# Reordering the small matrix products that stand behind the hidden rounds of a two-layer convolution kernel

## The chip, the core and the metric

The kernel runs on one core of a Trainium2 chip. The core has five engines that each work through a queue of their own: TensorE (PE in the profile, with its weight loads as PEld), VectorE (DVE), ScalarE (ACT), GpSimd (POOL) and SyncE (SP, which here only issues DMAs). Times are device microseconds of one execution. "Time" is the median of several executions; the profile is one further execution with the hardware profiler on.

## What is computed

The input x is 8 images (batch elements) of 8 channels and 512 x 512 values, all in 32-bit floats. Two residual layers follow each other.

```
# layer 0
v  = group_norm(x, 4 groups of 2 channels)
F  = rfft2(v[:, :, ::2, ::2]);  keep 8 x 4 low modes
G  = einsum('bixy,ioxy->boxy', F, w1 or w2)      # complex mixing of channels
x  = x + real(inverse transform of G at 512 x 512)
# layer 1
v  = group_norm(x)
grid = v
for _ in range(15):
    mapped  = 3.9 * grid * (1 - grid)
    grid    = 0.85 * (0.7 * mapped + 0.3 * conv3x3_depthwise(mapped)) + 0.15 * v
cml  = clip(grid)
nca  = sigmoid(conv1x1(relu(conv3x3(v, 8 -> 128)), 128 -> 8))
g    = sigmoid(conv1x1(relu(conv3x3([v, cml, nca], 24 -> 8)), 8 -> 8))
x  = x + g * cml + (1 - g) * nca
```

## The kernel before

The whole program is unrolled by a Python planner that writes every engine's instructions in one fixed order. Five kinds of work are interleaved.

- **Steps.** The 15-step loop runs on slabs of rows. `Slabs.convolve` (L535) writes one step as 48 matrix products into one half of PSUM; `Slabs.settle` (L548 on VectorE, L554 on ScalarE) reads the result and squares it. `settle` is called on two halves of a tile, so a step has two L548 instructions and two L554. After a step POOL issues small transfers (L581, L582) that renew the rows at the seams between slabs, and SP stores one row block (L591, `past`) for the last slab of a half.
- **Hidden rounds.** `Hidden.round` (L734) computes 128 hidden channels for 4 rows into one half of PSUM; ScalarE (L740) reads its first part and VectorE (L742) the second, into a tile `h`. `Hidden.point` (L761) multiplies `h` by the 1 x 1 weights; rounds in groups of four share one output tile `y`, which a ScalarE copy (L768) starts, VectorE adds to (L770), and a sigmoid closes (L773).
- **Gates.** A `Gate` handles 12 rows of the last stage. `load` issues six transfers on SP (three into `gin`, L796, and three into `mix`, L801). `conv` (L811, with L817 and L821 on VectorE and L816 on POOL), `point` (L828, with the sigmoid L832 on ScalarE and L834 on POOL) and `finish` (L839 on VectorE and the store L846 on SP) follow.
- **Layer 0 of the next element** is a generator, `layer0`. At each `yield` it names the kind of place at which its next piece may run. Its pieces are: statistics and the row transform of each of the 8 channels (`BATCH_NORM_STATS2` L332 on VectorE, products L338, copy L343); two averagings over partitions for the group norm (`group_stats`, L303 twice, with the square root L316 on ScalarE between its end and what follows); the column transform (L364); the complex mixing (`total`, L375 to L381, called once for the real part and once for the imaginary part, then L393 to L396, which fill `om`); and for each channel a product over rows (`over_rows`, L404, copied by L409), two products that add the result to x (`synthesis`, L437 and L440), new statistics (L457), and for each pair of channels a `close`: again two averagings, the square root, and the normalisation of both channels (L418, L421), after which they are stored.
- **The turn.** `work` emits one "tick": three steps, up to three hidden rounds, and then what stands behind the rounds. There are about 45 ticks for an element.

PSUM has eight banks, held as four pairs; two pairs make a half. Steps and rounds take the two halves in turn, so a step cannot begin to write a half before the step or round that used it last has been read by VectorE and ScalarE. Behind the rounds the names `first` and `second` stand for the two halves. If layer 0 has a WIDE piece (the synthesis) it takes the half that is next in turn, which becomes `second`, and `first` is the half of the last round. If not, `first` is the half of the round before last and `second` that of the last round. In both cases the next tick's first step writes `second`. (If two gates are convolved in a tick, it writes `first`.) Before the change the order behind the rounds is:

1. WIDE piece in `second`;
2. if the rounds belong to two groups, `point` of the older group in `first[1]`;
3. a gate's `conv` in `first[0]`, if one is loaded;
4. an EARLY piece of layer 0 in `second[0]`;
5. a second gate's `conv` in `second[0]`, if one is loaded;
6. `point` of the younger group in `first[1]`, a FILL piece (no PSUM);
7. up to two LATE pieces, in `second[1]` and `second[0]`;
8. `point` of the gates, then loads for further gates.

A closing's first averaging is EARLY and its second averaging is LATE. In the mixing, the real part is LATE and the imaginary part is EARLY one tick later; the first `over_rows` is LATE in that same tick.

`gates` is the number of gates to be loaded in a tick: 0, 1 or, when an element has more rows left than open ticks, 2. With 2, `work` loads one gate after the first step of the tick, and one at the tick's end. `shared.most` is the number of large buffers that gates and layer 0 may hold together: 4 as a rule, 3 near the ends of phases, and 7 from the sixth step slot of an element's first half to that half's end.

## Time and profile before

| What | Value |
|---|---|
| median of 3 runs | 9339.16 us (9327.55 to 9340.95) |
| the profiled execution | 9328.59 us, of which the span from the first to the last instruction is 9326.8 us |
| TensorE busy | 8776.0 us, 94% of the span |
| VectorE, ScalarE, GpSimd busy | 61%, 44%, 36% |
| mean granted TensorE clock | 0.987 |
| DMA | 1327 MB, mean 142 GB/s |

TensorE is the engine that sets the time: the span is its busy time and 551 us (9326.8 less 8776.0) of idle time, most of it in short pieces. A line of the waits view says which instruction waited, for whom, for how long in total, how often, and how long at most. A line of the timeline has the start and the length in us, the engine, the source line, what is written and read, the shapes and the number of instructions, and in brackets the idle time before the first of them with its releaser. One matrix product of the source stands as two records (103680 records for 1080 steps of 48 products), so the three steps of a tick are "x288".

### The profile page before, as it was taken

The page shows a single profiled execution, that of the slowest core. Times are in us where ns is not written, and L with a number is a line of the kernel's source. Part 1 is how long each engine was busy: PE and PEld are TensorE (multiplying, and loading weights), DVE is VectorE, ACT ScalarE, POOL GpSimd, SP SyncE. Part 2 cuts the span into 40 slices and gives each one's busy share as a digit, 9 for nine tenths or more (in the row PEclk, how much of TensorE's full clock was granted, in tenths as well). Part 3 has the DMA queues.
Part 4 walks back from the last instruction along what each step waited for, and adds up shares of the span by engine and source line. Part 5 has one row for each costly group of instructions (what it writes and reads, how often), then busy time and mean ns, then how long its engine had stood idle before and what let it go on. Part 6 is the DMA issues. An engine that isn't in the chain of part 4 may idle for free. (4 is left out here: it accounts for less than half of the span.)

```text
span 9326.8 us, 334742 instructions
## 1 busy us (share of the span) xinstructions
PE 8776.0 (94%) x150992; PEld 4165.1 (45%) x150992; DVE 5685.6 (61%) x5844; ACT 4101.0 (44%) x4285; POOL 3378.9 (36%) x4441
## 2 busy tenths in 40 slices
PE   5999999999999999999999999999999999899988
PEld 2445544444444444444444444444444444344433
DVE  5665567556665567655676556755567555555655
ACT  2445444444444444444444444444444444344422
POOL 3242334334343243433334343343433324453422
PEclk9999999999999999999999999999999999999999
DMA  5241356745566455754657546575455755665487
GB/s 158 79 127 39 96 150 167 171 109 152 148 178 146 112 155 145 184 137 112 169 146 176 129 108 167 156 179 126 111 158 167 173 117 129 144 153 119 105 212 184
DMA packets 697414, 1327.26 MB, mean 142 GB/s; under 512 B 146939, under 2 KB 152443, under 8 KB 668499
## 3 DMA queue, kind: packets, MB, share of 16 engines
q1 hardware_dynamic: 591840, 1244.38, 51.8%
q0 software_dynamic: 101792, 60.33, 3.0%
q8 instruction: 1187, 19.45, 0.9%
q14 instruction: 241, 1.97, 0.1%
q10 hardware_dynamic: 2354, 1.14, 0.0%
HBM read 977.48 MB, written 270.61 MB: 134 GB/s over the span
## 5 line engine op out<-in xcount | busy, mean ns | idle before, releaser
L535 PE MATMUL pair<-m,band 32*32 32x512 f32 x103680 | 3669.8, 605 | 205.2 <-issue 132.7
L554 ACT ACTIVATE m<-m 128x1024 f32<-128x1024 f32 x2016 | 2128.8, 1056 | 2081.0 <-DVE m L548 1994.9
L535 PEld LDWEIGHTS pair<-m,band 32*32 32x32 f32 x103680 | 2166.3, 103 | 1664.5 <-issue 820.3
L734 PE MATMUL pair<-cols,w_p 32*128 32x511 f32 (+1 forms) x24576 | 2800.1, 596 | 64.3 <-DMA cols<-xn 36.0
L734 PEld LDWEIGHTS pair<-cols,w_p 32*128 32x128 f32 x24576 | 1311.0, 185 | 1565.4 <-issue 1189.8
L548 DVE SCALAR_TENSOR_TENSOR m<-pair,dO 128x1024 f32<-128x1024 f32 x1152 | 1356.9, 1219 | 1040.0 <-PE pair L535 772.5
L581 POOL DMA_DIRECT2D m<-m x1568 | 855.3, 545 | 3061.0 <-ACT m L554 2983.1
L742 DVE TENSOR_SCALAR h<-pair,b_p 128x1024 f32<-128x1024 f32 x1024 | 1311.9, 1283 | 1045.4 <-PE pair L734 1035.3
L548 DVE SCALAR_TENSOR_TENSOR m<-pair,dE 128x1024 f32<-128x1024 f32 x1008 | 1187.3, 1219 | 867.3 <-PE pair L535 635.3
L740 ACT ACTIVATE h<-pair,b_p 128x1024 f32<-128x1024 f32 x1024 | 1141.2, 1115 | 1206.6 <-PE pair L734 1196.6
L834 POOL TENSOR_TENSOR mix<-mix 96x512 f32<-96x512 f32 x344 | 451.0, 1317 | 2010.8 <-ACT mix L832 1958.3
L761 PE MATMUL pair<-h,w_u 128*32 128x512 f32 x8192 | 999.0, 597 | 56.9 <-DVE y L770 30.4
L811 PE MATMUL pair<-gin,w_g 128*32 128x511 f32 (+1 forms) x8256 | 963.2, 604 | 64.5 <-DMA gin<-nca 45.8
L582 POOL DMA_DIRECT2D m<-m x1568 | 840.5, 536 | 36.7 <-issue 30.7
L811 PEld LDWEIGHTS pair<-gin,w_g 128*32 128x32 f32 x8256 | 254.3, 111 | 721.2 <-issue 654.8
L761 PEld LDWEIGHTS pair<-h,w_u 128*32 128x32 f32 x8192 | 246.2, 110 | 674.6 <-issue 516.5
L816 POOL TENSOR_TENSOR mix<-mix 96x512 f32<-96x512 f32 x344 | 446.4, 1300 | 191.0 <-DMA mix<-nca 143.5
L773 ACT ACTIVATE y<-y,b_u 128x512 f32<-128x512 f32 x256 | 184.9, 722 | 748.2 <-DVE y L770 747.9
L768 ACT COPY y<-pair 128x512 f32<-128x512 f32 x256 | 149.9, 586 | 693.3 <-PE pair L761 686.0
L558 POOL TENSOR_SCALAR dO<-dO 128x2048 f32<-128x2048 f32 x72 | 398.1, 5529 | 88.1 <-DVE m L548 87.0
L817 DVE SCALAR_TENSOR_TENSOR mix<-mix,back 96x512 f32<-96x512 f32 x344 | 379.7, 1104 | 81.0 <-DMA mix<-nca 63.9
L821 DVE TENSOR_SCALAR mix<-pair,b_g 128x512 f32<-128x512 f32 x344 | 257.2, 748 | 248.2 <-PE pair L811 238.2
(91 smaller groups left out, 3023.6 us busy)
## 6 DMA issues: line engine op xcount, KB each, us to landing
gin<-xn SPq DMA_DIRECT2D x344, 384.0 KB
cols<-xn SPq DMA_DIRECT2D x256, 512.0 KB
x<-in_x SPq DMA_DIRECT2D x120, 1024.0 KB
gin<-cml SPq DMA_DIRECT2D x344, 320.0 KB
gin<-nca SPq DMA_DIRECT2D x344, 320.0 KB
dE<-xn SPq DMA_DIRECT2D x288, 256.0 KB
dO<-xn SPq DMA_DIRECT2D x288, 256.0 KB
mix<-xn SPq DMA_DIRECT2D x344, 192.0 KB
```

Source lines behind the costliest of these rows:

```text
L535: nc.tensor.matmul(ps[h // 2][32 * t : 32 * t + 32, h % 2], band[at, self.channel(step - 1, h, t), dx], m[at, t, dx : dx + N], start=(n == ...
L548: nc.vector.scalar_tensor_tensor(u[:, at], ps[q], FLOOR, d[:, at], ALU.max, ALU.add)
L554: nc.scalar.square(u[:, at], u[:, at])
L581: nc.gpsimd.dma_start(out=view(tb, rb, dims), in_=view(ta, ra, dims))
L582: nc.gpsimd.dma_start(out=view(ta, ra + s, dims), in_=view(tb, rb + s, dims))
L734: nc.tensor.matmul(ps[g // 2][:, g % 2, lo:hi], w_p[p, dx, i % 2], self.cols[p, i // 2, at : at + hi - lo], start=(n == 0), stop=(n == 2), ...
L740: nc.scalar.activation(h[:, :2], ps[0], AF.Relu, bias=b_p)
L742: nc.vector.tensor_scalar(h[:, 2:], ps[1], b_p, 0.0, ALU.add, ALU.max)
L761: nc.tensor.matmul(ps[32 * g : 32 * g + 32], w_u[:, r % 4], h[:, g], start=(r == hs[0][0]), stop=(r == hs[-1][0]), tile_position=(0, 32 * g),)
L811: nc.tensor.matmul(ps[32 * j : 32 * j + 32, lo:hi], gband[:, dx], gin[:, j, at : at + hi - lo], start=(n == 0), stop=(n == 2), tile_positi ...
L816: nc.gpsimd.tensor_tensor(d, d, ng, ALU.subtract)
L834: nc.gpsimd.tensor_tensor(d, d, mix[: GR * C, 2], ALU.mult)
```

## The change

Five edits are made in one diff.

- A new kind of place, LAST, stands after the gates' `point`; its PSUM is `first[1]`, which the next step does not write. The second averaging of `group_stats` moves to it, at all five calls for each element. LATE keeps one place, `second[1]`.
- The mixing becomes one FILL piece: real and imaginary part and the filling of `om` follow each other in one tick. The first `over_rows` becomes EARLY in the next tick.
- If no gate is ready in a tick, the EARLY piece runs first of all, before the `point` of either group, and in `first[0]`. If one is ready the order is as before.
- `conv` of `Others` no longer tests whether a gate is ready; `ready` does.
- With `gates == 2` the load after the first step is made only while `shared.most < 6`. Else both gates are loaded at the tick's end.

```diff
 in group_stats, before the second averaging:
-        yield LATE, None
+        yield LAST, None
 in layer0:
-        yield LATE, None
+        yield FILL, None
         re = total(0, 0, 1, 1, ALU.subtract, "re")
-        yield EARLY, None
         im = total(0, 1, 1, 0, ALU.add, "im")
...
         nc.vector.scalar_tensor_tensor(to[:, :, 4:8], im, on_cos, back, ALU.mult, ALU.add)
-        yield LATE, None
+        yield EARLY, None
...
             if closing:
-                yield LATE, None
+                yield LAST, None
                 next(closing, None)
                 closing = None
...
-        for kind in (EARLY, LATE):
+        for kind in (EARLY, LAST):
             yield kind, None
             next(closing, None)
 in Others:
+        def ready(self):
+            if not self.loaded or now[0] < self.hold:
+                return False
+            return self.loaded[0].at + self.lag <= now[0]
+
         def conv(self, ps):
-            if not self.loaded or now[0] < self.hold or self.loaded[0].at + self.lag > now[0]:
-                return False
             g = self.loaded.popleft()
             g.conv(ps)
             self.convolved.append((g, ps))
-            return True
 in work:
-            if gates == 2:
+            if gates == 2 and shared.most < 6:
                 others.load(1)
                 gates = 1
...
         groups = e.hidden.sums()
+        gate = others.ready()
+        if not gate:
+            others.spectral(EARLY, [first[0][:, 0]])
         if len(groups) == 2:
             e.hidden.point(groups.pop(0), first[1][:, 0])
-        others.conv(first[0][:, 0])
-        others.spectral(EARLY, [second[0][:, 0]])
-        two = others.conv(second[0][:, 0])
+        two = False
+        if gate:
+            others.conv(first[0][:, 0])
+            others.spectral(EARLY, [second[0][:, 0]])
+            two = others.ready()
+            if two:
+                others.conv(second[0][:, 0])
         if groups:
             e.hidden.point(groups[0], first[1][:, 1])
         others.spectral(FILL, [None])
-        others.spectral(LATE, [second[1][:, 0], second[0][:, 0]])
+        others.spectral(LATE, [second[1][:, 0]])
         others.point()
+        others.spectral(LAST, [first[1][:, 0]])
         used[0] += two
```

In the order of the built programs, 49 of the 361 stretches between one tick's steps and the next differ on TensorE: five to seven in each of the seven elements that have a layer 0 beside them, and two in the last element, where the run of ticks with two gates starts one tick later and ends one tick later. The order on SP differs only in that last place, and the number of matrix products, transfers and VectorE operations is the same.

More of the change, by code (lines that the diff above doesn't have):

```diff
@@ L55 @@
 TICK = 3
-WIDE, EARLY, FILL, LATE = "wide", "early", "fill", "late"
+WIDE, EARLY, FILL, LATE, LAST = "wide", "early", "fill", "late", "last"
 GATES_FROM, SPECTRAL_FROM = 1, 0
```

## The prediction

> **What bounds the kernel now.** The page gives PE 8776.0 us of 9326.8: the sum of PE's work sets the time, and an edit that moves no work off PE can win only idle time, 551 us. So I read the waits of PE first, then timelines where they stand.

> ```profile
> engine line waited for: us in total, times, longest us
> PE pair L535 <- issue: 132.7, 83, 4.5
> PE pair L811 <- DMA gin<-nca: 45.8, 15, 5.8
> PE pair L535 <- ACT std L316: 40.0, 25, 2.7
> ...
> PE pair L303 <- DVE var L313: 34.1, 14, 12.2
> PE pair L761 <- DVE y L770: 30.4, 35, 1.2
> ```

> Three rows bear on the edits: std and var (the second averaging) and gin (gates). The next lines are a tick of a typical later element with a closing, in PE's, VectorE's and ScalarE's timelines. The LATE averaging (L303) wrote `second`, so L535 waits until ScalarE has loaded a table and taken the root.

> ```profile
> 5925.95 0.22 PE L303 MATMUL pair<-var,avg 128*32 128x1 f32 x8
> 5926.01 1.04 PE L828 MATMUL pair<-mix,w_g 128*32 128x512 f32 x6
> 5928.42 9.73 PE L535 MATMUL pair<-m,band 32*32 32x512 f32 x287 [1.36 <-ACT std L316]
> ...
> 5928.60 2.61 DVE L421 TENSOR_SCALAR x<-x,mean,rstd 128x2048 f32<-128x2048 f32 x2
> 5931.82 2.36 DVE L548 SCALAR_TENSOR_TENSOR m<-pair,dO 128x1024 f32<-128x1024 f32 x2 [0.62 <-PE pair L535]
> ...
> 5926.81 1.28 ACT L316 ACT_TABLE_LOAD   x1
> 5928.10 0.26 ACT L316 ACTIVATE std<-pair,eps 128x1 f32<-128x1 f32 x1
> 5928.38 1.28 ACT L832 ACT_TABLE_LOAD   x1
> 5929.68 0.69 ACT L832 ACTIVATE mix<-pair,b_g 96x512 f32<-96x512 f32 x1
> ```

> Next, a tick without a gate: L770 frees the bank for the second `point` before the statistics L332 begin.

> ```profile
> 5693.91 0.48 PE L338 MATMUL pair<-dft_y,x 128*32 128x32 f32 x32
> 5694.90 1.06 PE L761 MATMUL pair<-h,w_u 128*32 128x512 f32 x8 [0.51 <-DVE y L770]
> ...
> 5694.16 0.69 DVE L770 TENSOR_TENSOR y<-y,pair 128x512 f32<-128x512 f32 x1 [0.59 <-PE pair L761]
> 5694.76 4.84 DVE L332 BATCH_NORM_STATS2 st<-x 128x6 f32<-128x512 f32 x8
> ```

> Last, a two-gate tick of the last element, and the sums over it (PE, PEld, DVE, ACT, POOL, then granted clock, DMA share, GB/s): the first conv doesn't wait, the second does, and then takes twice as long.

> ```profile
> 8007.29 2.78 PE L811 MATMUL pair<-gin,w_g 128*32 128x512 f32 x24
> 8015.17 4.99 PE L811 MATMUL pair<-gin,w_g 128*32 128x512 f32 x24 [5.11 <-DMA gin<-nca]
> ...
> 7993.00:8021.00 28.00, 22.89 (x387) 10.01 (x383) 12.67 (x13) 8.72 (x9) 10.79 (x16) 0.88 0.64 149
> ```

> [...] 4.99 against 2.78 us for the same 24 records, clock 0.88. [...] The trace shows the 1.28 and no drain (the root follows 0.01 us later); I use 1.28.

> **The change, part by part.** The built order says what moves. Times are us.

> *Closings with a gate* (four for each of the six later elements). L828 now comes before L303, and L535 need not wait, so steps start 1.36 earlier (5927.06). But ScalarE now runs L832 (0.69) ahead of the table load, and nothing else has shortened: L828 ends 5927.05, L832 5927.8, load 5929.1, root 5929.4 instead of 5928.36. Behind it VectorE has L318 to L421 (2.83), and only then L548 of step 1 (2.36): done at 5934.6. Step 3 needs that half free. At 3.24 a step it could start at 5927.06 + 6.49 = 5933.55 and so waits 1.1. Before, it started at 5934.91. Of 1.36, 0.26 remains: the stall moves from step 1 to step 3. The closing at 5976 gives 0.6 of its 1.84 by the same working, the one at 6030 0.26. The last closing has L472 and L473 (1.5) behind L421 too: there PE loses 0.7 where the clock held (6089), and gains about 1.7 where the clock had fallen during the 2.7 wait for var (granted 0.5 around 1572); I take 0.5. Four together: +1.6.

> *Front averaging* (5798): the 0.68 on var and about 0.5 on the root go, 0.5 comes back at step 3: +0.6.

> *Mixing as one piece*: 12 small VectorE operations in two ticks become one block. im to `om` (5843.98 to 5846.62, 2.64) moves ahead of L548 one tick earlier, under step 1: settle 1 ends 28.7 after 5800, step 3 could start 28.4, cost 0.3. In the next tick the 1.79 of L404 on `om` goes; L828 then starts at 5845.9 for 5847.56, since L404 is already done: +1.65. Together +1.35.

> *EARLY first without a gate.* With rounds in one group (5715), L338 no longer waits 1.26 on L740, as `first` is an older half; but the row statistics L332 (2.47) hold L770, L773 and the copy L343 that frees `second`: +0.4 remains. With two groups (5694) it costs: in the built order L332 x4 (2.47 from 5693.57) now stands ahead of L770, which starts at 5696.03 for 5694.16. The second L761 waits for it: -1.87.

> Each later element: 1.6 + 0.6 + 1.35 + 0.4 - 1.87 = +2.1; six of them **+12**.

> *The first element's neighbour* has no gates, so L832 isn't in the way. By the same walk: two ticks with two groups -3.7; the waits of 1.26 at 234, 256 and 322 give 0.4, 1.2, 1.2; the front averaging at 306, whose root also waits behind L773, +3; first L404 +1.85 (1.41 on `om` and 0.4 of y); closings at 421, 476, 531 and 579. At 476 and 531 L303 waited 1.70 each for L440 on `second`, which `first` avoids, so the root itself comes 1.2 or more sooner; PE ran at half clock there (granted 0.5 near 421, 469, 476, 524). I take 2.3, 4, 4 and 0.5. Sum **+15**.

> *Two gates at the tick's end.* Six ticks (7967.89 to 8134.44, mean 27.8). Their waits on the second gin sum to 3.57 + 5.11 + 3.38 + 4.45 + 5.25 + 3.60 = 25.4. Half clock follows: each slow L811 costs up to 2.2, so the ceiling is about 39. On SP the twelve transfers of both gates now follow the two stores (which wait for L839, 6.5 after the tick begins) and `past` L591 (8009.53, 14.7 after). They carry 2 x (384 + 320 + 320 + 3 x 192) KB = 3.2 MB. The first conv comes 9.75 + 2.6 after the next tick begins, so about 18 after `past` in a 20-us tick. At 149 GB/s for a share of 0.64, full use would be 233, and 3.2 MB takes 14 at the least, 18 at 0.78 of that. That just fits; it isn't seen in the trace. From 5 (bound by transfers) to 39 (free); I take **+27**.

> *At nothing*: the `ready` test (Python); the prologue, where every queue keeps its order and only the rotation of banks differs; and the sigmoid table, which stood to be loaded again before L832 (5928.38) and is now loaded before the next tick's L773 or L832. There ScalarE idles (5.54 before L768 in the tick shown)[...]; uncovered, it would cost up to 1.28 in ticks where L828's bank is the next one written, and these are not among them. The closings' stores are issued a tick later as before, and SP's order is the same there, so no transfer moves but those of the gates. L834 on POOL comes with L832 some 2 sooner; L839 waits for it, which can only help.

> **Sum.** 12 + 15 + 27 = 54 off the profiled execution's 9328.6: 9274.6. That execution lies 10.6 below the median; off 9339.2 the sum is 9285. I predict **9286**.

> **Rivals.**
> - *A: the closings give all back and the two-group ticks decide.* [...] For: L421 is 2.61 and cannot move. Elements then give 0 instead of 27: 9339 - 27 = 9312.
> - *B: transfers bound the two-gate ticks.* For: share 0.64 already in 28-us ticks, 0.9 in 20. Against: slices of the page reach 212 GB/s. Gate gain 5: 9339 - 27 - 5 = 9307.
> - *C, slower: the gates' loads arrive late as a bunch.* Place: SP behind L591. If all twelve need over 27 us (122 GB/s; 121 was the lowest among these ticks), both convs wait. Each tick then loses 9 of wait and 2.3 of clock, six times 11.3 or 68 for the 39 before. It decides from about 11 a tick; with the elements at 5: 9339 + 29 - 5 = 9363.
> - *D: all gate stalls go and every half-clock stretch with them*: 39 + 40: 9260.

> **How the numbers follow.** Forecast 0.60 (9268 to 9306, run scatter in it), A 0.13, B 0.14, C 0.06, D 0.07. The range 9260 to 9322 leaves out C, half of D and the tails of A and of run scatter. 0.2% is 18.7 us, about what can be told from no change: faster means below 9320.5. Faster: 0.58 + 0.08 + 0.11 + 0.07 = 0.84; same 0.11; slower 0.05.

> **What would show it.** Right: L535 on std nearly gone, but new waits of L535 on VectorE's m (L548) or short gaps 6 to 7 us after a closing tick begins; L761 on y near 2.4 in the eight two-group ticks; L404 on `om` gone; two L811 groups of 2.7 back to back between 7990 and 8140, clock above 0.95. Wrong: if L535 after closings runs 288 records in 9.75 us with no stall, the closings are worth 30 us more than I say; if L811 waits on gin before the *first* conv of these ticks, B or C holds.

## The result

The changed kernel takes 9276.02 us (median of 5 runs, 9257.73 to 9298.59) where the kernel before took 9333.21 in the same comparison (5 runs, 9319.23 to 9340.95): a ratio of 0.9938, interval 0.9925 to 0.9952. A second, later comparison (`after_again`, below) gave 0.9956, 0.9941 to 0.9972. The forecast was 9286 in a range of 9260 to 9322.

Line numbers above 384 are one lower in the changed kernel: the steps are L534, `settle` L547, `point` L760, `y` L769, `conv` L810, the gates' `point` L827 and L831, the normalisation L420.

### The profile after

The waits view of the changed kernel, TensorE only (who waited, for whom, us in total, times, longest):

```profile
engine line waited for: us in total, times, longest us
PE pair L534 <- issue: 135.8, 75, 4.4
PE pair L760 <- DVE y L769: 46.7, 36, 2.3
...
PE pair L810 <- DMA gin<-nca: 15.0, 8, 3.5
PE pair L303 <- DVE var L313: 14.1, 2, 12.2
...
PE pair L534 <- DVE m L547: 11.0, 6, 1.8
...
PE pair L534 <- ACT mys L343: 7.0, 7, 1.0
...
PE pair L534 <- ACT std L316: 0.5, 1, 0.5
```

The three targets are gone or cut: std 40.0 to 0.5, var 34.1 to 14.1 (12.2 of it is one wait in the prologue), gin 45.8 to 15.0. Three rows show what was paid: `y` rose from 30.4 to 46.7, L534 waits for VectorE's `m`, which is a new row, and its wait for the copy L343 rose from 2.7 to 7.0. The row "issue", the largest of all, hardly moved; a later section returns to it.

Timelines of the changed kernel: first a closing tick on TensorE, ScalarE and VectorE, then a tick without a gate and with two groups (TensorE, then VectorE), then the steps and the two convs of a two-gate tick:

```profile
5898.99 0.60 PE L827 MATMUL pair<-mix,w_g 128*32 128x512 f32 x3
5899.04 0.22 PE L303 MATMUL pair<-var,avg 128*32 128x1 f32 x2
...
5899.99 10.93 PE L534 MATMUL pair<-m,band 32*32 32x512 f32 x288
...
5900.13 0.68 ACT L831 ACTIVATE mix<-pair,b_g 96x512 f32<-96x512 f32 x1 [0.31 <-PE pair L827]
5900.83 1.28 ACT L316 ACT_TABLE_LOAD   x1
5902.13 0.26 ACT L316 ACTIVATE std<-pair,eps 128x1 f32<-128x1 f32 x1
...
5902.62 2.60 DVE L420 TENSOR_SCALAR x<-x,mean,rstd 128x2048 f32<-128x2048 f32 x2
5905.14 2.35 DVE L547 SCALAR_TENSOR_TENSOR m<-pair,dO 128x1024 f32<-128x1024 f32 x2
...
5664.05 0.46 PE L338 MATMUL pair<-dft_y,x 128*32 128x32 f32 x32
...
5668.61 1.07 PE L760 MATMUL pair<-h,w_u 128*32 128x512 f32 x8 [2.34 <-DVE y L769]
...
5665.41 2.46 DVE L332 BATCH_NORM_STATS2 st<-x 128x6 f32<-128x512 f32 x4
5667.79 0.67 DVE L769 TENSOR_TENSOR y<-y,pair 128x512 f32<-128x512 f32 x1
...
7972.53 4.52 PE L534 MATMUL pair<-m,band 32*32 32x512 f32 x128 [2.57 <-issue]
7980.23 1.51 PE L534 MATMUL pair<-m,band 32*32 32x512 f32 x17 [3.18 <-issue]
...
7985.69 5.35 PE L810 MATMUL pair<-gin,w_g 128*32 128x512 f32 x48
```

In the closing tick the steps begin at once behind L827, without a wait in brackets, but the 288 records take 10.93 us where three steps that wait for nothing take 9.73 to 9.75. The records' own start times say where: the first pieces of step 3 (records 192, 194 and 196, counted from 0) start at 5906.41, 5906.86 and 5907.54, where the records just before them start hundredths of a microsecond apart. L547 frees them between 5906.3 and 5907.5. Each piece alone is too short for the waits view; only the length of the group betrays the wait. In the two-gate ticks both convs run as one group of 48 at 2.7 us for 24 records (granted clock 1.00), as the first conv of before (2.78 at 1.00). But the steps of this tick stop twice on "issue", for 2.57 and 3.18 us, where no step of these ticks stopped before.

The windows view (busy time of PE, PEld, DVE, ACT, POOL, then granted clock, DMA share, GB/s) over the two-gate ticks, before and after; the stretches are not the same work, so only the last three columns are compared:

```profile
7966.00:8133.00 167.00, 138.59 (x2324) 60.95 (x2312) 87.43 (x85) 55.84 (x59) 63.58 (x88) 0.92 0.63 144
```

```profile
7966.00:8125.00 159.00, 149.46 (x2776) 67.74 (x2746) 96.40 (x96) 65.18 (x68) 69.91 (x97) 0.99 0.68 166
```

The clock rose from 0.92 to 0.99, and the transfers ran faster, 166 GB/s for 144, so they were not at their limit before.

Laid tick against tick, the two traces differ as follows (gain in us). In what follows, the time of "the steps" runs from a tick's first L534 to the first record behind them (9.68 where nothing waits); "behind" is the rest, the rounds and what follows them.

| Stretch | Predicted | Measured |
|---|---|---|
| the first element's neighbour (18 ticks) | 15 | 21.1 |
| the two-gate ticks and those beside them (11 ticks) | 27 | 25.7 |
| six later elements (18 ticks each) | 12 | 11.4 |
| everything else | 0 | -5.6 |
| span | 54 | 52.6 |

The third row depends on where a stretch is cut, since stops on "issue" are scattered over it: with each stretch begun one tick earlier it is 17.6, and in the trace of `after_again` it is 6.7. The first row is 21.0 there, the second 20.2.

### The profile page after: what moved, and what is told of

It reads as the page before. It is cut to its first block, busy times and chain, and to the rows that moved or that the text cites. A ratio compares the mean times of both kernels' runs of the same rounds, so it can differ in the third digit from the quotient of the medians.

```text
span 9274.2 us, 334732 instructions
## 1 busy us (share of the span) xinstructions
PE 8786.8 (95%) x150992; PEld 4135.6 (45%) x150992; DVE 5669.4 (61%) x5844; ACT 4097.3 (44%) x4285; POOL 3374.3 (36%) x4441
## 3 DMA queue, kind: packets, MB, share of 16 engines
q8 instruction: 1187, 19.45, 0.9%
q14 instruction: 240, 1.97, 0.1%
## 5 line engine op out<-in xcount | busy, mean ns | idle before, releaser
L534 PE MATMUL pair<-m,band 32*32 32x512 f32 x103680 | 3694.5, 604 | 201.9 <-issue 135.8
L534 PEld LDWEIGHTS pair<-m,band 32*32 32x32 f32 x103680 | 2135.0, 103 | 1692.3 <-issue 833.4
L547 DVE SCALAR_TENSOR_TENSOR m<-pair,dO 128x1024 f32<-128x1024 f32 x1152 | 1356.0, 1218 | 1001.5 <-PE pair L534 794.2
L547 DVE SCALAR_TENSOR_TENSOR m<-pair,dE 128x1024 f32<-128x1024 f32 x1008 | 1186.4, 1218 | 878.5 <-PE pair L534 635.4
L833 POOL TENSOR_TENSOR mix<-mix 96x512 f32<-96x512 f32 x344 | 436.3, 1274 | 1932.8 <-ACT mix L831 1880.3
L760 PE MATMUL pair<-h,w_u 128*32 128x512 f32 x8192 | 997.7, 596 | 71.8 <-DVE y L769 46.7
L810 PE MATMUL pair<-gin,w_g 128*32 128x511 f32 (+1 forms) x8256 | 953.5, 598 | 34.7 <-DMA gin<-nca 15.0
L810 PEld LDWEIGHTS pair<-gin,w_g 128*32 128x32 f32 x8256 | 253.1, 110 | 685.8 <-issue 619.5
L760 PEld LDWEIGHTS pair<-h,w_u 128*32 128x32 f32 x8192 | 246.1, 109 | 686.9 <-issue 528.2
```

The lines of the kernel that those rows point to most:

```text
L534: nc.tensor.matmul(ps[h // 2][32 * t : 32 * t + 32, h % 2], band[at, self.channel(step - 1, h, t), dx], m[at, t, dx : dx + N], start=(n == ...
L547: nc.vector.scalar_tensor_tensor(u[:, at], ps[q], FLOOR, d[:, at], ALU.max, ALU.add)
L760: nc.tensor.matmul(ps[32 * g : 32 * g + 32], w_u[:, r % 4], h[:, g], start=(r == hs[0][0]), stop=(r == hs[-1][0]), tile_position=(0, 32 * g),)
L810: nc.tensor.matmul(ps[32 * j : 32 * j + 32, lo:hi], gband[:, dx], gin[:, j, at : at + hi - lo], start=(n == 0), stop=(n == 2), tile_positi ...
L833: nc.gpsimd.tensor_tensor(d, d, mix[: GR * C, 2], ALU.mult)
```

## The experiments

Two theories went in. The first, the **ledger** of the prediction: each wait that goes is mostly paid back at step 3, by L420 ahead of L547. The second, the **waits** theory: what leaves the waits view is won. Each of the four edits was first put alone into the kernel before (all on one chip, before 9331.78, median of 47 runs).

**e1_gates**: both gates loaded at the tick's end, nothing else.

```diff
-            if gates == 2:
+            if gates == 2 and shared.most < 6:
```

> The kernel before with the gates edit alone (both gates loaded at the tick's end where shared.most is 7). Theory of the prediction's ledger: all of it lies in the two-gate ticks of the last element, from about 7968 to 8135 us; L811's waits on gin there fall from 25 us to under 8, the clock there rises above 0.95, that stretch gets 22 to 28 us shorter, nothing else moves: about 9308 against 9333. Rival: transfers bound these ticks, and the gain of the changed kernel there needs the other edits: 5 us at most.

Measured 9303.3 us, ratio 0.9971 (0.9962 to 0.9980): about 27 us. In its single trace, as in that of the changed kernel, no wait for `gin` is left in the two-gate ticks, and these 11 ticks are 18.3 shorter. The loads' place alone removes the waits. Of rivals B (a gain of 5) and C (a loss) the numbers fall, though the steps of these ticks became longer, as the next section shows.

**e2_last**: the second averaging as LAST, nothing else.

```diff
-        yield LATE, None
+        yield LAST, None
...
-        others.spectral(LATE, [second[1][:, 0], second[0][:, 0]])
+        others.spectral(LATE, [second[1][:, 0]])
         others.point()
+        others.spectral(LAST, [first[1][:, 0]])
```

> The kernel before with the second averaging put last alone (LAST, in first[1]). Ledger: L535's wait on std goes (40 us to under 3), but in each closing with a gate step 3 then waits for step 1's settling, so the later elements gain about 2 to 4 us each and the first element's neighbour 5 to 8: 20 to 30 us in all, near 9308. Waits theory: what the waits view names is what is gained, std 40 and var 20 less the prologue's 12: 48 or more, near 9280.

Measured 9293.54 us, 0.9961 (0.9950 to 0.9973): about 36, between the two theories. In its trace the steps after the first closing last 10.86 in all six elements, as in the full change, so the payment is there; 14.2 come in the first neighbour and 16.1 in the later elements. The execution in the trace was the slowest of the 13 (9323.28), only 5 us below the profiled one of before: the other ticks lost 25. Rival A, the author's estimate that the closings give all back, falls by the median.

**e3_early**: `ready`, and the EARLY piece first in `first[0]` where no gate is ready.

```diff
+        gate = others.ready()
+        if not gate:
+            others.spectral(EARLY, [first[0][:, 0]])
         if len(groups) == 2:
             e.hidden.point(groups.pop(0), first[1][:, 0])
-        others.conv(first[0][:, 0])
-        others.spectral(EARLY, [second[0][:, 0]])
-        two = others.conv(second[0][:, 0])
+        two = False
+        if gate:
...
```

> The kernel before with the early piece first where no gate is ready, alone. Ledger: eight two-group ticks lose 1.9 us each (L761 on y L770, from 0.5 to 2.4), ten one-group ticks win 0.4 to 1.3, two closings win the 1.7 on L440: between -8 and +8 in all, not to be told from no change by time. Rival: moving the early piece off the bank of the last round is a clean gain, 10 to 20 us faster.

Measured 9335.35 us, 1.0001 (0.9990 to 1.0013): nothing. A two-group tick loses 1.80 behind its rounds (mean of six), a one-group tick wins 1.33 there, and the first neighbour wins 4.0. A gain and a loss of the same edit cancel.

**e4_mix**: the mixing as one FILL piece, the first `over_rows` as EARLY.

```diff
-        yield LATE, None
+        yield FILL, None
         re = total(0, 0, 1, 1, ALU.subtract, "re")
-        yield EARLY, None
         im = total(0, 1, 1, 0, ALU.add, "im")
...
-        yield LATE, None
+        yield EARLY, None
```

> The kernel before with the mixing as one piece alone. Ledger: the waits of L404 on om (12 us, 7 times) go and the stretch behind the rounds gets 1.7 to 2 shorter, but the steps of the tick in which the block now runs get 0.3 to 1.4 longer, since the settling of step 1 stands behind it: 0.6 to 1.4 gained for each of seven elements, 4 to 10 us, not told by time alone. Rival: VectorE has room under step 1, steps stay at 9.75, and 13 us or more are gained.

Measured 9313.67 us, 0.9984 (0.9975 to 0.9993): about 15. In each of the six later elements 2.00 go behind the rounds of one tick and 0.72 come back in the steps of the tick with the block (10.40 for 9.68); with 6.1 in the first neighbour that makes 6 x 1.28 + 6.1 = 14. That is more than the 4 to 10 expected, but 4.7 of the 6.1 stand at the first neighbour's closings, whose order this edit leaves alone.

The four ratios add up to about 77 us (27 + 36 - 1 + 15), more than the change gave (58, or 41 in the second comparison). One part of the difference is seen in the next section: in the full change the mixing block costs 1.35 and not 0.72, six times 0.6. The rest wasn't settled; each of the four carries some 10 us of uncertainty.

Next, three edits to the changed kernel, each against one payment (before 9323.28 on this chip, 7 runs). The changed kernel itself was not run beside them, so what they gain over it is a difference of two ratios, here against 0.9938. It is uncertain by some 18 us, and against 0.9956 it would be 17 larger each time.

**i1_order**: without a gate, the older group's `point` first and the EARLY piece behind it.

```diff
-        if not gate:
-            others.spectral(EARLY, [first[0][:, 0]])
         if len(groups) == 2:
             e.hidden.point(groups.pop(0), first[1][:, 0])
+        if not gate:
+            others.spectral(EARLY, [first[0][:, 0]])
```

> The changed kernel with one thing undone: where no gate is ready and the rounds are in two groups, the older group's point comes first again and the early piece after it, still in first[0]. Ledger: the eight two-group ticks get the 1.8 us back that they lost, L760 on y falls from 47 to about 31 us, one-group ticks and closings keep what they won: 14 us less than the changed kernel, near 9262 where that gives 9276. Rival: L760 then waits elsewhere, the stretch behind the rounds stays as long, no change.

Measured 9247.88 us, 0.9921 (0.9906 to 0.9935). Timeline of its TensorE in the two-group tick:

```profile
5650.60 0.48 PE L338 MATMUL pair<-dft_y,x 128*32 128x32 f32 x32
5651.69 1.07 PE L760 MATMUL pair<-h,w_u 128*32 128x512 f32 x8 [0.61 <-DVE y L769]
```

The wait for `y` is 0.61 for 2.34, the row `y` is back at 30.4, and in the later elements these ticks are 1.97 shorter each. Eight such ticks make 16 us; the ratios give about 16 too, and the ledger said 14.

**i2_root**: the LAST piece ahead of the gates' `point`, so that ScalarE takes the root before the sigmoid L831.

```diff
-        others.point()
         others.spectral(LAST, [first[1][:, 0]])
+        others.point()
```

> The changed kernel with the last piece put ahead of the gates' point (still in first[1]), so that ScalarE takes the root before the gate's sigmoid. Ledger: the root comes 0.7 us or more sooner, the step-3 stall of closings falls: the steps after a closing, 10.85 us now, take 10.0 to 10.3, the stretch behind the rounds stays within 0.3; 8 to 15 us less in all. Rival: the 10.85 comes from something else (transfers, the clock), and the steps stay at 10.85.

Measured 9242.22 us, 0.9916 (0.9897 to 0.9934), about 20 better than the change. ScalarE of i2_root in a closing tick:

```profile
5884.96 1.28 ACT L316 ACT_TABLE_LOAD   x1
5886.26 0.26 ACT L316 ACTIVATE std<-pair,eps 128x1 f32<-128x1 f32 x1
5886.53 1.28 ACT L831 ACT_TABLE_LOAD   x1
```

The root ends 1.33 after the steps begin (5885.19 to 5886.52), where in the changed kernel it ends 2.40 after (5899.99 to 5902.39); the steps after the first and third closings take 9.88 for 10.85 in seven of twelve cases, and 10.2 to 11.9 in the others. It also shortens a tick that has no closing: that of the mixing block. There the changed kernel's ScalarE, VectorE and GpSimd do this:

```profile
5794.69 1.28 ACT L831 ACT_TABLE_LOAD   x1 [5.77 <-PE pair L827]
5795.99 0.68 ACT L831 ACTIVATE mix<-pair,b_g 96x512 f32<-96x512 f32 x1
...
5795.20 0.41 DVE L379 TENSOR_TENSOR ts<-ts 16x256 f32<-16x256 f32 x1
...
5797.06 1.39 DVE L379 TENSOR_TENSOR ts<-ts 16x256 f32<-16x256 f32 x1
...
5799.85 2.34 DVE L547 SCALAR_TENSOR_TENSOR m<-pair,dE 128x1024 f32<-128x1024 f32 x2
...
5796.75 1.42 POOL L833 TENSOR_TENSOR mix<-mix 96x512 f32<-96x512 f32 x1 [6.68 <-ACT mix L831]
```

ScalarE was idle for 5.77 us, and still the load didn't run in that time: it waited for L827, as the ACTIVATE behind it does. So L831 came 1.28 later, and L833 fell on the second L379, which ended only after L833 (1.39 for 0.41), and L547 came late for step 3. In i2_root the sigmoid table is already in place in this tick, no load is there, and the steps take 10.40 for 11.02 in all six elements.

**i3_split**: only the even channel is normalised ahead of the steps; the odd one (L420 and, in the last closing, L472 and L473) follows the three steps of the next tick, as a new kind NORM.

```diff
             for c in (2 * g, 2 * g + 1):
+                if c % 2:
+                    yield NORM, None
                 xt = e.x[C + c]
                 nc.vector.tensor_scalar(xt, xt, mean, rstd, ALU.subtract, ALU.mult)
...
         others.finish()
+        others.spectral(NORM, [None])
```

> The changed kernel with each closing's second normalisation (one L420 of 1.3 us) and, in the last closing, L472 and L473 moved from ahead of step 1's settling to behind the three steps. Ledger: VectorE then settles step 1 in time: the steps after a closing with a gate fall from 10.85 to 9.7 to 9.8 us unless instruction stalls fill the place, those after the last closing from 14.0 to 10.5 or less; 20 to 40 us less in all. Rival: step 3 is late for another reason than VectorE's queue, and nothing moves.

Measured 9260.54 us, 0.9933 (0.9918 to 0.9948): about 5 better than the change where 20 to 40 were expected, a miss by these ratios. Its VectorE (L422 is the normalisation here, L554 `settle`) and TensorE (L541 the steps), closing tick and next tick:

```profile
1394.34 1.35 DVE L422 TENSOR_SCALAR x<-x,mean,rstd 128x2048 f32<-128x2048 f32 x1
1395.60 2.35 DVE L554 SCALAR_TENSOR_TENSOR m<-pair,dO 128x1024 f32<-128x1024 f32 x2
...
1391.71 9.75 PE L541 MATMUL pair<-m,band 32*32 32x512 f32 x288
...
1417.81 6.44 PE L541 MATMUL pair<-m,band 32*32 32x512 f32 x176
1427.45 5.56 PE L541 MATMUL pair<-m,band 32*32 32x512 f32 x82 [3.20 <-issue]
```

The mechanism answered: with half of the normalisation out of the way the steps after the first and third closings are back at 9.75 (ten of twelve), without a wait at step 3. The time did not follow. The tick shown after it stops for 3.20 on "issue", a stop that no semaphore explains; over the six elements the ticks after the steps of the first and second closings grew by 2.4 and 1.35 on the mean, and the row "issue" by 15 us (151.0 for 135.8).

**i4_both**: i1_order and i3_split together.

> The changed kernel with both edits of the two runs before (the order of two-group ticks, and the split normalisation). Ledger: the two add up, 35 to 55 us less than the changed kernel, near 9230; faster than the kernel before by about 1%. Rival: one hides the other, and less than 25 us come.

Measured 9235.91 us, 0.9909 (0.9894 to 0.9924), about 27 better than the change: within the scatter what i1_order and i3_split give singly, 16 + 5, and less than the 35 to 55 expected.

Last, the two orders together and all three, with the changed kernel beside them on one chip (before 9325.63, 11 runs).

**after_again**: the changed kernel, unchanged.

> The changed kernel as it is, beside the next two on one chip, as their measure. Ledger and rival alike: 0.994 of the kernel before; the steps after a gated closing 10.85 us again.

Measured 9278.41 us, 0.9956 (0.9941 to 0.9972). The steps take 10.85 after closings and 11.02 beside the mixing block, as in the first trace.

**b1_order_root**: i1_order and i2_root.

> The changed kernel with two edits: the older point first in two-group ticks, and the last piece ahead of the gates' point. Ledger: they touch different ticks and add, 16 and 20 us less than the changed kernel: 30 to 40 less, about 0.990 of the kernel before. Rival: instruction stalls fill the place as they did behind the split normalisation, and less than 25 come.

Measured 9245.12 us, 0.9916 (0.9900 to 0.9933): 33 below the changed kernel. It beats both kernels.

**b2_all**: i1_order, i2_root and i3_split.

> The same two edits and the split normalisation. Ledger: with the root early step 3 is late by little, so the split adds nothing but the last closing's 1 us for each element and brings its instruction stalls in the tick after: within 8 us of the kernel with two edits. Rival: the split adds its 5 us or more.

Measured 9237.44 us, 0.9916 (0.9900 to 0.9932). Splitting the normalisation adds nothing that can be told from b1_order_root.

## Why the prediction was right, and where it was not

The total was right, and so was the mechanism of most terms. That the total came so near is in part luck: a loss that the prediction had no term for was met by a cautious choice, and several small terms were mis-sized, in both directions.

- **Two gates at the tick's end**: +27 predicted, 25.7 in the trace, 27 from e1_gates alone. The number agrees, and the working does not. In the seven ticks from 7968 to 8151 the waits for `gin` fall from 25.4 us to none, and behind the rounds 38.6 are won: the whole ceiling of 39. But the steps of these ticks became 13.2 longer. Before, none of them stopped on "issue"; now they stop for 8.7, and behind the stop of 3.18 the granted clock is 0.5 for 3.41 us (from 7980.79). All nine traces with this edit show it: 37.7 to 39.8 won behind the rounds, 10.7 to 19.7 lost in the steps. The prediction knew no such loss. Its 27, taken between 5 and 39, met the difference by luck, and part of what rival B feared came by another way. The half clock behind these waits, which the ceiling of 39 counts, stands in five of six cases: before, the second L811 took 4.43 to 5.34 at a mean granted clock of 0.50 to 0.62, behind waits of 3.38 to 5.25; in the sixth, behind a wait of 3.60, it took 2.78 at 1.00. Now that these waits are gone the clock over the ticks is 0.99 for 0.92.
- **Closings with a gate**: the stall moves from step 1 to step 3, as worked out. The three gated closings before the last win 1.46, 2.04 and 1.46 behind the rounds (predicted 1.36, 1.84 and 1.36); the steps then take 1.17 more, and 1.24 after the second (predicted 1.1). That i2_root and i3_split shorten exactly these steps shows the chain root, L420, L547. The ledger compared with steps that stop nowhere, though, and they did stop: before, the steps after these three closings took 10.75, 11.04 and 10.58 on the mean over the six elements, because of stops on "issue", and 10.85, 11.99 and 10.86 after. After the first and third closings the new stall mostly took the place of a stop that was there, and the real payment was 1.3 for the three together instead of 3.6.
- **The last closing**: +0.5 predicted, about -0.7 found. Its term was mis-sized: the gain behind the rounds is 0.2, while the steps grew by 0.87 on the mean (13.44 to 14.31), since L472 and L473 stand ahead of L547 as well. These are the six waits of 1.8 in the new row `m`.
- **Front averaging**: +0.6 predicted, 0.64 found.
- **Mixing as one piece**: the gain was 2.00 for 1.65, but step 3 pays 1.35 for 0.3: +0.65 net for +1.35. Two assumptions failed. The sum took the durations of VectorE's operations from the trace of before, where they stood clear of GpSimd; beside L833 some are longer. In e4_mix and i2_root two L375 take 1.09 for 0.74; that is half of the 0.72 there, and the other half is near the 0.3 predicted. And ScalarE's idle time did not cover the load of the sigmoid's table: the load stands right before the ACTIVATE it belongs to (5794.69 and 5795.99), and waited 5.77 us for L827 with it. So L833 came later and cost L379 0.98 instead of L375 0.35. That adds 0.62, and i2_root removes exactly that. The L379 that began beside L833, at 5797.06, ended at 5798.45, 0.28 after L833 did (5798.17); why an operation is longer there was not shown.
- **EARLY first without a gate**: -1.87 predicted in a two-group tick, -1.82 in most of them, -1.80 alone in e3_early. In one-group ticks +0.4 predicted; 1.33 came behind the rounds, and about 0.6 was lost in the steps, because L534 waits for the copy L343 (7.0 us in seven waits, 2.7 before): +0.7.
- **The first neighbour**: +15 predicted, 21.1 found. The term too low is that of the closings: 10.8 predicted, 17.4 found. All the other terms together make 3.9 predicted, 3.6 found. About 3 of the 17.4 may belong to the profile of before and not to the edits: e1_gates, which changes nothing in this stretch, also shows 1.6 and 1.7 less behind the rounds of two of these ticks.

With the stalls counted in full, the corrected terms make +0.9 for each later element (-1.82 + 0.7 + 0.64 + 0.65 + 4.96 - 3.58 - 0.7), 5 for six; with the real payment of 1.3 at the closings they make 19. Measured were 11.4 in one trace and 6.7 in the other. So the agreement with the 12 predicted is luck. What lies between was not found tick by tick; the likely cause is stops on "issue", which fall elsewhere from trace to trace (the two traces of the same kernel differ by 4.7). The prediction had no term for these stops; they are the largest idle row, and they decide what a small edit is worth here.

What stays open: why the four edits singly add up to 77 us, and how much the stops on "issue" take back outside the two-gate ticks. Each tick-by-tick account rests on one execution of a kernel, two for the changed one.

## What to carry to other kernels

When an edit removes a wait ahead of a chain of work, walk the chain to the next buffer that must come free and count what now stands in that engine's queue; here a stall of 1.17 followed two steps behind a gain of 1.46, and it showed only as a longer group without brackets. Ask also what ran under the old wait: when 39 us of waits went from the two-gate ticks, 11 to 20 came back as steps that stopped where they had not before. A table load did not fill idle time here (ScalarE idled 5.77 us, then loaded for 1.28): put the instruction with the other function where the reload falls behind work that nobody waits for. And let an operation that frees a bank go ahead of long work in the same queue, even if the long work could start sooner: `y` before the statistics was worth 1.97 us in each such tick.

## What the runs showed of the hardware

```profile
q8 instruction: 1187, 19.45, 0.9%
```

19.45 MB in 1187 packets are 16.4 KB each, and the 303963 instructions of the trace make 1187 blocks of 256. The packet records show the wait itself. In the kernel before, a packet takes about 1.1 us. Where no stop follows (732 boundaries in the steps), it starts 0.7 us (median) after TensorE passed the boundary before, and it has landed 2.7 us (median, never under 1.2) before TensorE reaches the next one. At the 83 stops it starts 3.9 us after (median), and TensorE goes on 1.2 to 1.7 us after it has landed. By these times the stops are waits for a block of instructions.

Why a packet starts late is less certain. The windows of the kernel before, 8 us ahead of a stop (1.37 us at 5939.52) and 8 us of steps without one:

```profile
5931.00:5939.00 8.00, 7.15 (x221) 4.65 (x190) 6.40 (x7) 4.23 (x4) 3.58 (x6) 1.00 0.95 316
5900.00:5908.00 8.00, 8.00 (x237) 5.31 (x238) 5.88 (x9) 3.61 (x5) 1.28 (x1) 1.00 0.45 115
```

Over all of these boundaries (83 and 732), the DMA share in the 8 us ahead was 0.87 (224 GB/s) where a block's boundary brought a stop, and 0.53 (134 GB/s) where it brought none. So the likely cause, in the author's estimate from these shares, is that the packet queues behind the kernel's own transfers. It is a correlation in the traces; no run changed the transfers alone to prove it. It would explain why i3_split won so little. Ahead of its stop of 3.20 us TensorE passed a boundary at 1419.04, the next packet started only at 1424.71 and landed at 1425.86, and TensorE went on at 1427.45. A window over that time has a share of 0.94:

```profile
1418.00:1424.00 6.00, 6.00 (x176) 3.39 (x153) 2.91 (x4) 2.12 (x3) 1.28 (x1) 1.00 0.94 193
```
